# Input statistics placed at another silu, and three of four ring loads issued back to back, in a Mamba and FFN kernel with a planned order

## The chip, the cores and the metric

The kernel runs on one core of one Trainium2 chip. The metric is the device time of one execution in microseconds. Before the change the median of three runs is 4940.54 us (4936.31 to 4943.96).

## What is computed

The input x has 4 sequences of 2048 tokens of 256 numbers. A layer norm is taken, a Mamba block (with a layer norm and a residual of its own) is applied to it and added to x, and a gated feed-forward part follows on another layer norm. Cut to what matters:

```python
def _mamba_block(x, ...):
    residual = x
    xn = (x - mu) * rsqrt(var + 1e-05) * ln_w + ln_b
    xi, z = split(xn @ W_in, 2)                  # 512 channels each
    u = silu(causal_conv(xi, conv_w) + conv_b)   # 4 taps
    dt_r, Bm, Cm = split(u @ W_xproj)            # 16, 64, 64
    delta = softplus(dt_r @ W_dt + b_dt)
    A = -exp(A_log)
    def step(h, inputs):                         # over the 2048 tokens
        dA = exp(d_t[:, :, None] * A)
        h = h * dA + (d_t * u_t)[:, :, None] * B_t[:, None, :]
        return h, einsum('bdn,bn->bd', h, C_t)
    y = (scan(step) + u * D) * silu(z)
    return residual + y @ W_out

x = x + _mamba_block(layernorm(x), ...)
n = layernorm(x)
x = x + (silu(n @ wg.T) * (n @ wu.T)) @ wd.T     # hidden width 768
```

The state has 512 channels times 64 entries, so per token 32768 recurrences run in parallel: 256 rows of 128.

## The kernel before

**Tiling.** The 8192 tokens are cut into 16 blocks of 512 (`NT`, four to a sequence). In a block the 32768 recurrences are 256 pairs (two channels times 64 states on the 128 partitions), in 16 groups of 16. One pair goes through these steps:

- PE spreads delta of two channels over the partitions into one of four `a` buffers in PSUM (line 1528, from the tile `stk`).
- ACT takes the exponential in place, with the pair's row of A as the scale (line 1534).
- DVE runs the recurrence over 512 tokens with one scan instruction (line 1539), in place in a `ring` buffer that holds delta times u times B.

Ahead of the scans, the ring buffer of a group (16 pairs by 512 tokens) is loaded from a scratch tensor `dusc` in DRAM by four loads of four pairs each (`load_du`, line 1494; the first group's first load is split in three), and POOL multiplies it with B in two halves of eight pairs (line 1645). Behind the scans PE contracts the group's states with C (line 1563), and then the buffer is free. There are three ring buffers.

**The dense parts.** While the scans of block n run, the dense work of its neighbours is woven in. In program order it is: `front(n+1)` (load of x, its layer norm, xn and its transposes), `back(n-1)` (gating and output projection), `front_a(n+1)` (projection and convolution), `front_b(n+1)` (the z projection by `project_z`, the silu of u and z at lines 998 to 1001, softplus, the stores for the scans), `back_b(n-1)` (feed-forward, with its silu at lines 1265 to 1267). Silu lies in another table of ACT than the exponential, so each of the two silu stretches begins and ends with a table load, and ACT takes no exponential in between.

**The norm of x.** `layer_norm` with `twice=True` gives the scale and shift of both layer norms in front of the Mamba block from one pair of statistics. Its steps are: four `bn_stats` on DVE (line 491), which read the loaded x and write one of four `bst` buffers each; four `bn_aggr` on DVE (line 492), which write into a PSUM bank `lp`; small ACT steps (two of line 530, lines 540, 541, 542) and three tiny DVE steps (lines 545, 550, 555). x itself stays in a `w4` buffer until it is normalised.

**What sets the order.** No engine order is written by hand. Every instruction is an `op` with a planned cost, and `Planner.run` puts them one by one on PE, ACT, DVE, POOL and SP as it simulates the engines; the resulting orders are emitted, and an instruction waits on the chip only for what its data need. Instructions of the scan chain have kind "S"; dense ones have kind "D" and a `step` at which they are due, spread over the block by cost (`dense`, line 1628): being early or late by some steps shifts a candidate's planned time by at most 170 ns later or 230 ns earlier (`bias`, line 222). Buffers are given out in turns: the four `w4` buffers in program order over everything, the four PSUM `ps` banks in program order among the dense instructions, which also need two free ones (`allocatable`, line 155). In `w4`, the turns of a block are x, xn, xnT, the residual of `back`, two z buffers, then the residual of `back_b` (loaded at line 1224), its xn, xT and the second part of the hidden tile.

All transfers are issued by SP in one order, and a transfer that must wait holds up those behind it. `wire` is the planned time at which everything issued so far has been moved. Transfers of kind "S", the ring loads and the `stk` loads, are not planned earlier than 3 us before that (lines 238 and 239, `AHEAD` = 3000 ns); dense transfers have no such rule. The four loads of a ring buffer are also chained by `after=[last["du"]]`, each behind the start of the one before.

Of the kernel before, what the change touches and what calls it, by code (L numbers as in the profile page):

```python
# [93 lines left out]
class Planner:  # L94
# [114 lines left out]
    def run(self, mul):  # L209
# [17 lines left out]
        while left:  # L227
            best = None
            for e, now in clock.items():
                pick = None  # L230
                cands = []
                due = 1e18
                for o in self.ready[e]:
                    t = self.allocatable(o, 2)
                    if t is None:
                        continue
                    t = max(now, o.est, t)
                    if e == "SP" and o.kind == "S":
                        t = max(t, wire - AHEAD)
                    if o.kind == "S":  # L240
                        due = min(due, t)
                    cands.append((o, t))
                for o, t in cands:
                    late = HOLD if e in HOLD_ON and o.kind != "S" and t + o.cost > due + HOLD_TOL else 0.0
                    sc = (t + bias(o) + late, o.idx)
                    if pick is None or sc < pick[0]:
                        pick = (sc, t, [o])
                if self.ready["MUL"] and (e == "POOL" or e == "DVE" and min(o.idx for o in self.ready["MUL"]) < self.dve_mul):
                    m = min(self.ready["MUL"], key=lambda o: o.idx)
                    whole = m.key[0][0] == 0 or MUL_SET == sum(o.key[0] == m.key[0] for o in self.ready["MUL"])  # L250
                    if e == "POOL":
                        ms = sorted(
                            (o for o in self.ready["MUL"] if o.key[0] == m.key[0]), key=lambda o: o.idx
                        )
                        ms = [o for i, o in enumerate(ms) if o.key[2] == m.key[2] + i]
                        sc = 0.0
                    else:
                        ms = [m]
                        sc = max(LAG, min(MUL_LEAD, SLOPE * (m.step - MUL_MARGIN - cur)))
                    t = max(now, max(o.est for o in ms))  # L260
                    sc = (t + sc, m.idx)
                    if whole and (pick is None or sc < pick[0]):
                        pick = (sc, t, ms)
                if pick and (best is None or pick[1] < best[1]):
                    best = (e, pick[1], pick[2])
            assert best, "no instruction can be placed"
            e, t, os = best
            if os[0].eng == "MUL":
                cost = 88 + 1092 * len(os) if e == "POOL" else 690
                mul(e, os)  # L270
                clock[e] = end = t + cost
                busy[e] += cost
                for o in os:
                    self.ready["MUL"].remove(o)
                    o.eng = e
                    self.commit(o, t, end)
                left -= len(os)
                continue
            o = os[0]
            self.ready[e].remove(o)  # L280
            cost, times = o.cost, 1
            if e == "PE":
                i = int(t / TICK)
                if cols.get(i - 1, 0) < WARM:
                    cost *= 2
                if was == "decay" and o.key == "narrow":
                    cost += SWITCH
                was = o.key
                n = o.cols or o.cost * 2.4
                while recent and recent[0][0] < t - TICK:  # L290
                    recent.popleft()
                if o.key == "decay" and sum(c for _, c in recent) < KEEP:
                    times = 2
                    cost *= 2
                    n *= 2
                recent.append((t + cost, n))
                i = int((t + cost) / TICK)
                cols[i] = cols.get(i, 0) + n
            if e == "SP":
                clock[e] = t + 625  # L300
                wire = max(wire, t + 1275) + o.cost
                end = wire + 985
                busy[e] += o.cost
            else:
                clock[e] = end = t + cost
                busy[e] += cost
            if o.key == "scan":
                cur += 1
            self.commit(o, t, end)
            for _ in range(times):  # L310
                o.fn()
            left -= 1
# [26 lines left out]
def mamba_ffn_kernel(  # L339
# [124 lines left out]
            one(s)  # L464
        return sums

    def layer_norm(src, blocks=range(4), twice=False, sums=None):

# [17 lines left out]

        def stats(j, s):
            st = buf("bst")  # L490
            op("DVE", 326, lambda: nc.vector.bn_stats(st.t, tok(src)[:, s, :]), [(src, s // 2)], [st])
            op("DVE", 205, lambda: nc.vector.bn_aggr(mv()[:, j, :], st.t), [st], [(lp, 0, j)])

        def spread(s):
# [277 lines left out]
    def front(n):  # L772
        r = n % R
        xt = load_x(n) if n else x0
        rs, nm = layer_norm(xt, twice=True)
        rp = buf("s4")
        op("ACT", 180, lambda: nc.scalar.activation(rp.t[:, 0:4], rs.t[:, 0:4], AF.Copy, bias=1.0), [rs], [rp])
        xn = buf("w4")
        normalise(xn, xt, (rs, nm), o=4)

        def keep():
            normalise(xt, xt, (rp, nm))
            store(rsum[r], lambda: tok(xt), 524288, halves(xt), [("rsum", r)])

        if n:
            keep()
        else:
            last["keep"] = keep
        xnT = buf("w4")

        def ev_t(c):
            def ev(ps):
                op(
                    "ACT", act(T, True, 2),
                    lambda: nc.scalar.activation(  # L795
                        xnT.t[:, c, :], ps.t, AF.Identity, bias=lnb[:, c : c + 1], scale=lnw[:, c : c + 1]
                    ),
                    [ps, "lnw", "lnb"], [(xnT, c)],
                )

            return ev

        for c in range(2):
            transposes(xn, c, ev_t(c))
        rest[n] = xnT
# [66 lines left out]
    def project_z(n):  # L872
        xnT = rest[n][0]
        szs = gates[n] = [buf("w4"), buf("w4")]

        def ev_z(k):
            def ev(ps):
                op(
                    "ACT", act(T, True), lambda: nc.scalar.copy(szs[k // 2].t[:, k % 2, :], ps.t),
                    [ps], [(szs[k // 2], k % 2)],  # L880
                )

            return ev

        for k in range(4):
            project(win, DI + k * P, xnT, ev_z(k), ["win"])

    def mix(n):
        r = n % R
# [98 lines left out]
    def front_b(n):  # L988
# [2 lines left out]
        uk = [(u, k) for k in range(4)]  # L991
        if n:
            project_z(n)
            szs = gates[n]
            zk = [(z, k) for z in szs for k in range(2)]

            def silu():
                nc.scalar.activation(u.t, u.t, AF.Silu)
                for h in range(2):
                    nc.scalar.activation(szs[h].t, szs[h].t, AF.Silu)  # L1000
                nc.scalar.preload_act_table_set(EXP_LN)

            o = op("ACT", 6400, silu, uk + zk, uk + zk)
            o.tail = -1283.0
            for k in uk:
                o.tails[k] = -3250.0
        else:

            def silu_a():
                nc.scalar.activation(u.t[:, 0:3, :], u.t[:, 0:3, :], AF.Silu)  # L1010

            def silu_b():
                nc.scalar.activation(u.t[:, 3, :], u.t[:, 3, :], AF.Silu)
                nc.scalar.preload_act_table_set(EXP_LN)

            op("ACT", 2900, silu_a, uk[0:3], uk[0:3])
            op("ACT", 1900, silu_b, uk[3:4], uk[3:4]).tail = -1283.0
# [461 lines left out]
    def group(G):  # L1479
# [14 lines left out]
        def load_du(a, m):  # L1494
            src = dusc[r][h][:, row + a : row + a + m, :].rearrange("d p t -> d (p t)")
            o = load(
                lambda: ring.t[:, a : a + m, :].rearrange("p a t -> p (a t)"),
                src[None, :, :].to_broadcast([64, 2, m * T]),
                m * 262144,
                r=[("dusc", r, h, 0), ("dusc", r, h, 1)],  # L1500
                w=keys[a : a + m] + heads[(a + 3) // 4 : (a + m + 3) // 4],
                after=[stl] if G == 0 and a == 4 else [last["du"]] if "du" in last else [],
            )
            last["du"] = o

        def mul(p):
            o = op("MUL", 0, None, [b2, keys[p]], [keys[p]], step=G * 16 + p)
# [210 lines left out]
```

## Time and profile before

| What | us |
|---|---|
| median of three runs | 4940.54 |
| profiled execution, time | 4944.55 |
| profiled execution, span | 4942.8 |
| DVE busy | 4734.0 |
| POOL busy | 4695.2 |
| PE busy | 4433.3 |
| ACT busy | 4005.2 |

The span is the time from the first to the last instruction of the profiled execution; the time of that execution is 1.75 us longer. A row of the groups names line, engine, operation and tiles, then the count, the busy time, the mean duration in ns, and the idle time of the engine just ahead of these instructions with what ended most of it. Scans overlap a little: one lasts 1198 ns, and they follow each other at 1115 ns. In a timeline, the columns are start and length in us, and a bracket tells how long the engine had been idle and what released it. "issue" as a releaser means that the profile shows no wait.

Some further groups that the text refers to:

| Group | count | busy us | mean ns |
|---|---|---|---|
| line 491, `bn_stats`, DVE | 68 | 23.9 | 410 |
| line 492, `bn_aggr`, DVE | 68 | 11.7 | 171 |
| line 998, table load, ACT | 15 | 19.2 | 1283 |
| line 998, silu of u, ACT | 15 | 28.7 | 1911 |
| line 1000, silu of z, ACT | 30 | 29.8 | 1041 |
| line 1265, silu of the gate, ACT | 15 | 28.7 | 1913 |

| Transfer | count | KB | median us from issue to landing |
|---|---|---|---|
| ring<-dusc | 1023 | 1024 | 7.9 |
| stk<-dsc | 256 | 96 | 5.9 |
| szd<-w | 32 | 512 | 11.6 |
| qd<-w | 32 | 512 | 9.5 |
| w<-rsum | 31 | 512 | 8.3 |

### The profile page before, as it was taken

What the parts mean: (1) busy time and instruction counts of PE and PEld (TensorE: products, weight loads), DVE (VectorE), ACT (ScalarE), POOL (GpSimd) and SP (SyncE); (2) the same over time, 40 slices, a digit from 0 to 9 for tenths busy, and PEclk for the clock granted to TensorE, in tenths of its full rate; (3) what the DMA queues carried; (4) which work ended last, traced back from release to release, by engine and by line L of the source; (5) the groups of instructions that cost most, each with busy time, mean ns of one, the idle gap of its engine ahead of it and who ended that gap; (6) DMA issues with size and microseconds to landing.
All of it is one profiled execution on the core that took longest, in us unless ns stands there. A gap on an engine that the chain in (4) does not pass through costs nothing. (4 is left out here: it accounts for less than half of the span.)

```text
span 4942.8 us, 116006 instructions
## 1 busy us (share of the span) xinstructions
PE 4433.3 (90%) x46924; PEld 2205.2 (45%) x46924; DVE 4734.0 (96%) x4576; ACT 4005.2 (81%) x7378; POOL 4695.2 (95%) x862
## 2 busy tenths in 40 slices
PE   7889989998988999989999899989989999898888
PEld 3434444444444444444444444444444444444435
DVE  7999999999999999999999999999999999999996
ACT  6788878778788887888878788887878878888774
POOL 6999999999999999999999999999998999999994
PEclk9999999999999999999999999999999999999999
DMA  8676776667766777677667676677776767676762
GB/s 295 237 282 252 284 272 266 265 242 287 265 266 257 272 266 280 263 266 279 262 264 278 259 277 255 263 291 267 274 263 247 280 265 282 255 290 253 264 248 86
DMA packets 306347, 1299.87 MB, mean 263 GB/s; under 512 B 33617, under 2 KB 134737, under 8 KB 174866
## 3 DMA queue, kind: packets, MB, share of 16 engines
q1 hardware_dynamic: 305810, 1292.44, 68.6%
q8 instruction: 369, 6.05, 0.5%
q14 instruction: 168, 1.38, 0.1%
HBM read 1186.94 MB, written 105.38 MB: 261 GB/s over the span
## 5 line engine op out<-in xcount | busy, mean ns | idle before, releaser
L1539 DVE TENSOR_TENSOR_SCAN ring<-a,ring 128x512 f32<-128x512 f32 x4096 | 4594.2, 1198 | 103.7 <-ACT a L1534 81.2
L1645 POOL TENSOR_TENSOR ring<-ring,b 128x4088 f32<-128x4088 f32 (+2 forms) x512 | 4540.0, 8897 | 154.3 <-DMA ring<-dusc 116.9
L1534 ACT ACTIVATE a<-a,a 128x512 f32<-128x512 f32 x4096 | 2702.2, 666 | 677.2 <-PE a L1528 647.1
L1528 PE MATMUL a<-stk,selb 128*128 128x512 bf16 x5088 | 1809.3, 391 | 407.4 <-DVE ring L1539 374.7
L1563 PE MATMUL ps<-ring,cz 128*32 128x128 f32 x32768 | 1235.9, 280 | 19.4 <-issue 12.4
L1528 PEld LDWEIGHTS <-selb 128*128 128x128 bf16 x5088 | 471.2, 98 | 1347.6 <-issue 1274.2
L1563 PEld LDWEIGHTS ps<-ring,cz 128*32 128x32 f32 x32768 | 811.1, 110 | 541.4 <-issue 478.0
L596 PE MATMUL ps<-w,wgu 128*128 128x512 f32 x720 | 373.5, 600 | 0.0
L1584 ACT COPY mm<-ps 128x512 f32<-128x512 f32 x512 | 304.5, 596 | 37.2 <-PE ps L1563 36.3
L1597 PE MATMUL ps<-mm,exs 128*32 128x128 f32 (+1 forms) x4112 | 285.3, 407 | 1.3 <-ACT mm L1584 1.0
L596 PE MATMUL ps<-w,win 128*128 128x512 f32 x512 | 260.7, 594 | 0.3 <-ACT w L795 0.3
L830 PE MATMUL ps<-xi,w 128*128 128x512 f32 x480 | 245.8, 593 | 0.0
L1597 PEld LDWEIGHTS ps<-mm,exs 128*32 128x32 f32 x4112 | 116.8, 118 | 202.8 <-ACT a L1534 81.6
L1148 PE MATMUL ps<-wd,w 128*128 128x256 f32 x720 | 195.8, 386 | 0.0
L596 PEld LDWEIGHTS ps<-w,wgu 128*128 128x128 f32 x720 | 138.1, 192 | 111.2 <-issue 58.5
L1148 PEld LDWEIGHTS ps<-wd,w 128*128 128x128 f32 x720 | 132.4, 189 | 42.1 <-issue 14.7
L949 PE MATMUL ps<-w,ident 128*128 128x512 f32 x248 | 133.3, 620 | 6.7 <-ACT ps L944 5.9
L596 PEld LDWEIGHTS ps<-w,win 128*128 128x128 f32 x512 | 96.8, 190 | 89.7 <-issue 57.5
L1148 PE MATMUL ps<-wout,w 128*128 128x256 f32 x480 | 128.4, 388 | 0.9
L830 PEld LDWEIGHTS ps<-xi,w 128*128 128x128 f32 x480 | 88.9, 188 | 82.6 <-issue 62.2
L571 ACT ACTIVATE w<-w,s,s 128x256 f32<-128x256 f32 x192 | 112.8, 597 | 0.9 <-DVE s L555 0.9
L1255 POOL TENSOR_TENSOR w<-w,w 128x512 f32<-128x512 f32 x90 | 113.4, 1281 | 0.0
(154 smaller groups left out, 2416.9 us busy)
## 6 DMA issues: line engine op xcount, KB each, us to landing
ring<-dusc SPq DMA_DIRECT2D x1023, 1024.0 KB, 7.9
stk<-dsc SPq DMA_DIRECT2D x256, 96.0 KB, 5.9
qd<-w SPq DMA_DIRECT2D x32, 512.0 KB, 9.5
szd<-w SPq DMA_DIRECT2D x32, 512.0 KB, 11.6
dusc<-w SPq DMA_DIRECT2D x63, 256.0 KB, 6.4
dsc<-pk SPq DMA_DIRECT2D x63, 256.0 KB, 6.5
rsum<-w SPq DMA_DIRECT2D x31, 512.0 KB, 6.8
w<-rsum SPq DMA_DIRECT2D x31, 512.0 KB, 8.3
```

The source lines that it names most:

```text
L596: lambda ps: nc.tensor.matmul(ps, w[:, c, o : o + P], xT.t[:, c, :], start=(c == 0), stop=(c == 1)),
L830: lambda: nc.tensor.matmul(ps.t, dg.t[:, j * P : (j + 1) * P], xi.t[:, j : j + T], start=(j == 0), stop=(j == 3)),
L949: lambda: nc.tensor.matmul(ps.t, m, t.t, start=False, stop=True, skip_group_check=True),
L1148: lambda ps: nc.tensor.matmul(ps[:, (s % 2) * DM : (s % 2 + 1) * DM], src(k)[:, s * P : (s + 1) * P], w[:, k, :], start=False, stop=(k == ...
L1255: "POOL", 1230, lambda: nc.gpsimd.tensor_tensor(hm(k), hm(k), up.t, ALU.mult),
L1528: "PE", 216, lambda: nc.tensor.matmul(a.t, selb[:, p, :], stk.t, start=True, stop=True),
L1534: lambda: nc.scalar.activation(a.t, a.t, AF.Exp, scale=a2f[:, idx : idx + 1]), [a, "a2"], [a],
L1539: nc.vector.tensor_tensor_scan(v, a.t, v, 0.0, ALU.mult, ALU.add)
L1563: nc.tensor.matmul(pm.t[cg * 32 : cg * 32 + 32, (r8 % 4) * P : (r8 % 4 + 1) * P], framed(cz, blk), ring.t[:, :, blk * 8 : blk * 8 + 8], st ...
L1584: nc.scalar.copy(mm.t[:, hb * 4 : hb * 4 + 4].rearrange("p r a t -> p (r a t)"), pm.t)
L1597: nc.tensor.matmul(ex.t[jh * 32 : jh * 32 + 32, a * 16 : b * 16], framed(exs, jh * 2 + jl), mm.t[:, a:b, :, jh * 2 + jl], start=(jl == 0), ...
L1645: e.tensor_tensor(v, v, b2.t[:, None, t0:].to_broadcast([P, m, T - t0]), ALU.mult)
```

## The change

It has two parts.

The first moves the load of x and the layer norm's statistics of a block. In `front_b` of block n, right behind the z projection and ahead of the silu in program order, x of block n + 1 is loaded and its `layer_norm` is planned. The statistics may be placed from the start of the last z matmul on. `front(n+1)` then takes the finished scale and shift from a table and starts with the normalising. It applies to blocks 2 to 15; block 0 has no silu of that kind, so block 1 keeps the old place.

The second exempts the later loads of a ring buffer from the rule of 3 us: loads with `a` other than 0 get the key "more", which the planner asks for. The first load of a group and the `stk` load keep the rule.

```diff
@@ class Planner, run @@
-                    if e == "SP" and o.kind == "S":
+                    if e == "SP" and o.kind == "S" and o.key != "more":
                         t = max(t, wire - AHEAD)
@@
-    def layer_norm(src, blocks=range(4), twice=False, sums=None):
+    def layer_norm(src, blocks=range(4), twice=False, sums=None, after=()):
...
         def stats(j, s):
             st = buf("bst")
-            op("DVE", 326, lambda: nc.vector.bn_stats(st.t, tok(src)[:, s, :]), [(src, s // 2)], [st])
+            op("DVE", 326, lambda: nc.vector.bn_stats(st.t, tok(src)[:, s, :]), [(src, s // 2)], [st], after=after)
@@ front @@
         xt = load_x(n) if n else x0
-        rs, nm = layer_norm(xt, twice=True)
+        rs, nm = norms.pop(("in", n), None) or layer_norm(xt, twice=True)
@@ project_z @@
         for k in range(4):
-            project(win, DI + k * P, xnT, ev_z(k), ["win"])
+            last["z"] = project(win, DI + k * P, xnT, ev_z(k), ["win"])[-1]
@@ front_b @@
         if n:
             project_z(n)
+            if n + 1 < NT:
+                xt = load_x(n + 1)
+                norms["in", n + 1] = layer_norm(xt, twice=True, after=[last["z"]])
             szs = gates[n]
@@ group, load_du @@
             last["du"] = o
+            if a:
+                o.key = "more"
```

## The prediction

> **What bounds the kernel now.** I read the page first, then the table of waits, then the timeline around the two long ACT stretches of a block.
>
> From the page, the busy time of each engine and the two costliest groups:
>
> ```profile
> PE 4433.3 (90%) x46924; PEld 2205.2 (45%) x46924; DVE 4734.0 (96%) x4576; ACT 4005.2 (81%) x7378; POOL 4695.2 (95%) x862
> L1539 DVE TENSOR_TENSOR_SCAN ring<-a,ring 128x512 f32<-128x512 f32 x4096 | 4594.2, 1198 | 103.7 <-ACT a L1534 81.2
> L1645 POOL TENSOR_TENSOR ring<-ring,b 128x4088 f32<-128x4088 f32 (+2 forms) x512 | 4540.0, 8897 | 154.3 <-DMA ring<-dusc 116.9
> ```
>
> DVE sets the pace: 4096 scans, and only 4942.8 - 4734.0 = 208.8 us idle in the whole span. POOL is nearly as full, so the waits must say who waits for whom:
>
> ```profile
> DVE ring L1539 <- ACT a L1534: 81.2, 43, 4.9
> ...
> DVE ring L1539 <- POOL ring L1645: 0.3, 1, 0.3
> ...
> POOL ring L1645 <- DMA ring<-dusc: 116.9, 41, 31.6
> ```
>
> (Total us, times, longest.) A scan waited for POOL once, 0.3 us. POOL waits for ring loads, 31.6 us of it once at the start, but its product is there in time anyway. What DVE does wait for is ACT, in waits of up to 4.9 us. The timeline around the silu of a block ahead (line 998) shows why; first DVE, then ACT, then SP:
>
> ```profile
> 2913.82 5.66 DVE L1539 TENSOR_TENSOR_SCAN ring<-a,ring 128x512 f32<-128x512 f32 x5
> 2923.63 3.45 DVE L1539 TENSOR_TENSOR_SCAN ring<-a,ring 128x512 f32<-128x512 f32 x3 [4.16 <-ACT a L1534]
> ```
>
> ```profile
> 2916.52 1.28 ACT L998 ACT_TABLE_LOAD   x1
> ...
> 2921.64 1.28 ACT L1001 ACT_TABLE_LOAD   x1
> ```
>
> ```profile
> 2911.93 0.51 SPq L425 DMA_DIRECT2D ring<-dusc  x1
> 2912.55 0.99 SPq L425 DMA_DIRECT2D stk<-dsc  x1
> 2913.94 0.51 SPq L425 DMA_DIRECT2D ring<-dusc  x1
> 2914.52 0.57 SPq L425 DMA_DIRECT2D w<-rsum  x1
> 2915.21 1.18 SPq L425 DMA_DIRECT2D ring<-dusc  x2
> ```
>
> For 6.4 us ACT makes no exponential. DVE uses up the ones it has, and from S + 2.95 to S + 7.11 (S = 2916.52) it stands still: a hole of 4.16 us. The fifteen holes at line 998 are 2.76 to 4.89 us, 62.6 us together. On SP, other transfers go between the four loads of one ring. The other silu of a block (line 1265), on DVE, and its last occurrence, which has no next block:
>
> ```profile
> 2403.10 6.77 DVE L1539 TENSOR_TENSOR_SCAN ring<-a,ring 128x512 f32<-128x512 f32 x6
> 2409.79 1.38 DVE L491 BATCH_NORM_STATS2 bst<-w 128x6 f32<-128x256 f32 x4
> 2412.85 2.34 DVE L1539 TENSOR_TENSOR_SCAN ring<-a,ring 128x512 f32<-128x512 f32 x2 [1.68 <-ACT a L1534]
> ```
>
> ```profile
> 4741.36 2.34 DVE L1539 TENSOR_TENSOR_SCAN ring<-a,ring 128x512 f32<-128x512 f32 x2 [3.04 <-issue]
> ```
>
> This is the view that decides. The four statistics (line 491) **already lie in a hole**: 1.68 + 1.38 = 3.06, the 3.04 of a silu without them. Only their aggregations lie on the path, some 85 us later:
>
> ```profile
> 2494.24 0.16 DVE L492 BATCH_NORM_AGGREGATE ps<-bst 128x2 f32<-128x6 f32 x1
> 2494.31 1.19 DVE L1539 TENSOR_TENSOR_SCAN ring<-a,ring 128x512 f32<-128x512 f32 x1
> 2495.42 0.17 DVE L492 BATCH_NORM_AGGREGATE ps<-bst 128x2 f32<-128x6 f32 x1
> 2495.49 1.19 DVE L1539 TENSOR_TENSOR_SCAN ring<-a,ring 128x512 f32<-128x512 f32 x1
> 2496.60 0.39 DVE L492 BATCH_NORM_AGGREGATE ps<-bst 128x2 f32<-128x6 f32 x2
> 2496.90 2.32 DVE L1539 TENSOR_TENSOR_SCAN ring<-a,ring 128x512 f32<-128x512 f32 x2
> ```
>
> From 2494.24 to 2496.90 are 2.66 us with two scans of pitch 1.115 (four aggregations between them): 2.66 - 2.23 = 0.43 us a block.
>
> **Part one, the statistics.** No instruction is added or removed. For blocks 2 to 15 the load of x, four statistics, four aggregations and the eight small ACT and DVE steps of the norm move from the start of the next dense part to the silu at line 998. Block 2's four statistics are already in that hole (2.76 us left at 246.7, as 4.14 less 1.38); the thirteen others come from the hole at line 1265. Leaving that one gains nothing: it grows from about 1.5 to 2.9 us. Going into the other costs nothing while it lasts: the start of the trace shows such statistics with three of the four aggregations in 1.75 us (78.17 to 79.92); with a fourth of 0.17 they take 1.9 of the 4.2 us. So what can be gained is the aggregations: 14 x 0.43 = 6.0 us, not the 14 x 1.9 = 27 us that the empty hole suggests. The three tiny DVE steps (0.14 us each) need ACT after the silu and stay on the path.
>
> If the cover is gone, that is, if x lands after S + 7.11, the four statistics go between scans: they add 1.38 a block to the 0.43 paid today, 14 x 1.38 = 19.3 us. x is late from S + 7.11 - 1.92 = S + 5.2 on. Its load takes the turn in the w4 buffers right after the second z buffer, where line 1224's load (w<-rsum) is now: issued at 2914.52, S - 2.0, with 8.3 us to landing (the page's median) it comes at S + 6.3, half too late. In 8 of the 13 blocks the third z copy is 3.3 to 3.5 us ahead of the silu, like here; in five it is some 11 us ahead, and x is in time. What speaks for in time: planned work of about 4.5 us (the load 1344, statistics 2124, small steps 1080 ns) now stands behind z instead of ahead of it in an order that spreads some 200 us over 236 steps, so z falls due about 5 steps, 5 to 6 us, earlier. On PE the last z matmuls are cut off from the first by a burst of line 1563 (at 1999.69 to 2006); a few 1.1-us places are enough to bring them ahead of it, with the load ahead of the ring loads too. That is an estimate.
>
> The x tile also holds one of four w4 buffers through the back of the block, so line 1224's load waits for the last z matmul and the normalise at line 571 (2930.83, S + 14.3) for a szd store (11.6 us from its issue near S + 4.2: S + 15.8). A delay of 1 to 2 us in a chain with room (its last dusc store of one block is issued at 2085.97, the next block's first stk load at 2163.99): I take nothing, and up to 2 us over the run. The mean's bank (lp) comes before line 1024's banks in PSUM turns: line 1024 is late if x is late.
>
> **Part two, the loads.** Three of each group's four loads (c1 to c3; 256 groups) are issued right behind the first, ahead of whatever SP held between them: stk, bcs, qd, szd, dusc, dsc, rsum, x. Nothing is added on the wire. A load of 1024 KB at the 401 GB/s that the window from 2915 to 2924 shows takes 2.6 us, so a transfer that loses its place behind c2 and c3 lands 5.2 us later, behind three 7.8. Gain: POOL waits less, worth 0.3 us steady, and at most 3 us at the start, where DVE is idle 22.7 of the 60 us from 30 to 90. Loss: ACT's waits for a buffer's store or load are 18.5 (yl<-qd), 15.4 (dusc<-w) and 11.2 us (dsc<-pk); were they doubled, DVE would feel about what it feels of ACT outside the silus, 9.5 us. So -3 to +10; I take 0, since the first loads, which POOL's first half needs, hardly move, and stk lands 8.9 us or more ahead of its first matmul once the first group is past.
>
> What a page says on the order of transfers is a check on this: the row is the 96-KB stk load with 5.9 us to landing, so it is the queue that takes the time. The Trainium skill (DMA: Bandwidth & Descriptors, section on queues, rings and completion order) says that each DMA engine consumes a queue's descriptors in ring order. By it a load of x behind c1 to c3 can't overtake them and the sum is +19; by the row of w<-rsum alone, placed among the ring loads, it is between -6 and +8.
>
> **The sum.** The profiled run took 4944.55 us (span 4942.8), 4.0 above the median of 4940.54. 4944.55 - 6.0 + 0 = 4938.5; against the median 4934.5. Forecast: **4935 us**, its own range 4927 to 4943.
>
> **The rivals.** *x comes late* (slower). At the silu of line 998 the load stands behind c1 to c3, lands after S + 7.1, and the statistics lie between scans while line 1265's hole stays empty. With the phases of today in 8 blocks: 8 x 1.38 - 6 x 0.43 = +8.5, 4949; in all: +19.3, 4960. It decides from a landing at S + 5.2. For it: part two itself, and the eight blocks. Against: z falls due earlier. I take 4953.
>
> *Statistics ahead of the silu.* If x is early and the dense part is late, the statistics go before the silu, between scans: 1.38 + 0.43 on the path, of which a fuller stock of exponentials (one scan, 1.1) comes back: 0.7 against 0.43 today, 14 x 0.27 = +4, 4944.
>
> *A shorter hole.* DVE does only 2.4 to 3.1 us of scans after S, though four a buffers hold 4.46. Should the new order start the silu with one exponential more in stock, that is 14 x 1.1 = 15 us on top of 6: 4919. For it: holes differ by 0.7 us among blocks by their phase. Against: today's order never reaches it.
>
> **How the numbers follow.** Chances: forecast 0.40, late 0.34, ahead 0.10, shorter 0.16. No change is within 0.2%, 9.9 us, about what a measurement of this kernel can tell. The forecast gives 0.16 of its 0.40 to faster (with gains of part two and a reshuffled order, below 4930.6) and 0.24 to same; late 0.32 slower and 0.02 same; ahead 0.08 same, 0.02 slower; shorter 0.16 faster. So faster 0.32, same 0.34, slower 0.34. The range goes from 4916, just below the shorter hole, to 4962, late in all blocks with part two's small losses: less than one in ten is left out on each side.
>
> **What would show it.** Right: at line 998 statistics and aggregations inside the hole, which leaves about 2.3 us; at line 1265 holes of about 3; no aggregation between scans. Wrong: line 491 between scans right after line 1001, with the load of x landing beyond S + 7; or holes at line 998 under 1.5 us; or DVE waiting for POOL or PE for stk, which would mean that part two is not neutral.

## The result, and the profile after

| Kernel | median us | ratio to the kernel before, 95% interval |
|---|---|---|
| before | 4938.43 | |
| after | 5070.25 | 1.0266 (1.0253 to 1.0279) |

With a fourth run the median of the kernel before is 4938.43 us instead of 4940.54. The change costs 131.8 us. Lines behind 994 have moved down by three and five: the silu of the block ahead is at lines 1001 to 1004, the feed-forward's at 1268 to 1270, the scan at 1544, its exponential at 1539, POOL's product at 1650.

The page of the changed kernel: busy times of the engines, and DVE's busy tenths over the span.

```profile
PE 4419.6 (87%) x46638; PEld 2223.2 (44%) x46930; DVE 4739.6 (94%) x4576; ACT 4007.4 (79%) x7378; POOL 4695.8 (93%) x862
...
DVE  7999899999989989999998999999999898999996
```

DVE does the same work (4739.6 us against 4734.0) and stands still 5062.5 - 4739.6 = 322.9 us instead of 208.8. Six slices, spread over the span, fall from nine tenths to eight. The granted clock of PE is lower too (0.964 against 0.976), but a scan lasts what it did (1199 ns against 1198), and the largest wait for PE, ACT's for the spread delta (line 1528, now 1533), fell from 647.1 us to 636.0; so the clock is not what costs the time. What ACT waits for, first before the change, then after (total us, times, longest), and then what DVE waits for after it:

```profile
ACT w L942 <- DMA dusc<-w: 15.4, 11, 3.6
...
ACT pk L956 <- DMA dsc<-pk: 11.2, 8, 3.9
```

```profile
ACT w L942 <- DMA dusc<-w: 90.3, 20, 7.8
ACT pk L956 <- DMA dsc<-pk: 45.8, 7, 10.5
```

```profile
DVE ring L1544 <- ACT a L1539: 113.6, 76, 5.4
DVE w L957 <- ACT x L961: 41.4, 22, 10.5
...
DVE ps L545 <- ACT ps L542: 31.7, 16, 2.7
DVE w L957 <- ACT pk L956: 27.1, 14, 5.6
```

Both ACT lines are in softplus. Each takes a buffer that a store to DRAM still reads, so ACT waits for that store to land: 136.1 us in all, against 15.4 + 11.2 = 26.6 before. DVE's multiplication at line 957 then waits for ACT 68.5 us (17.7 before), and the scans wait more too. The 31.7 us at line 545 are no loss: nearly all of them lie inside the silu's hole, as will be seen.

Where DVE stands still, summed from the idle time in front of its instructions in each trace. "Silu" is around the table loads, "softplus" from 7 to 105 us behind the start of the silu of the block ahead, "start" the first 100 us, "end" the last 70:

| us | start | silu | softplus | rest | end |
|---|---|---|---|---|---|
| before | 34.7 | 86.0 | 16.7 | 27.2 | 40.6 |
| after | 36.5 | 85.6 | 149.2 | 7.7 | 40.6 |

The softplus stretch loses 132.5 us, the rest gives 19.5 back, and nothing else moves by over 2 us (the span grew by 119.7). In the softplus stretch DVE is idle for 4 to 15 us in 13 of the 15 blocks and for about 1 in the other two. One place of it in the changed kernel's timeline (start, length; in brackets the idle time before and who ended it), SP first, then ACT, then DVE:

```profile
1774.50 2.48 SPq L425 DMA_DIRECT2D ring<-dusc  x4
```

```profile
1782.92 0.33 SPq L428 DMA_DIRECT2D dusc<-w  x1
1783.34 0.38 SPq L425 DMA_DIRECT2D stk<-dsc  x1
1784.54 0.37 SPq L428 DMA_DIRECT2D dsc<-pk  x1
```

```profile
1782.94 0.26 ACT L962 COPY x<-w 128x64 f32<-128x64 f32 x1
...
1789.96 0.63 ACT L942 ACTIVATE w<-w 128x512 f32<-128x512 f32 x1 [5.44 <-DMA dusc<-w]
1790.50 0.64 ACT L1539 ACTIVATE a<-a,a 128x512 f32<-128x512 f32 x1
```

```profile
1782.81 4.55 DVE L1544 TENSOR_TENSOR_SCAN ring<-a,ring 128x512 f32<-128x512 f32 x4
1791.17 2.34 DVE L1544 TENSOR_TENSOR_SCAN ring<-a,ring 128x512 f32<-128x512 f32 x2 [3.80 <-ACT a L1539]
```

The four loads of a ring buffer go out in one go, as part two wants. By the trace the last of them lands at 1789.30, and the small transfers issued behind it follow in the order of their issue: the dusc store at 1789.88, stk at 1790.12, the dsc store at 1790.80. ACT needs the store's buffer for its next instruction and stands still until 1789.96, 5.44 us. Its last exponential ended at 1784.00 and the next ends at 1791.14; of these 7.14 us DVE bridges 3.36 with the scans it still has (to 1787.36) and waits 3.80 us. Over the run a dusc store takes 9.4 us from issue to landing (6.4 before), and 26 of the 63 are issued while all four loads of a group are under way; before, none.

At the silu of the block ahead (here S = 1731.05) it went as predicted:

```profile
1731.82 0.73 DVE L491 BATCH_NORM_STATS2 bst<-w 128x6 f32<-128x256 f32 x2
1732.46 0.40 DVE L492 BATCH_NORM_AGGREGATE ps<-bst 128x2 f32<-128x6 f32 x2
1732.77 0.39 DVE L491 BATCH_NORM_STATS2 bst<-w 128x6 f32<-128x256 f32 x1
1733.08 1.20 DVE L1544 TENSOR_TENSOR_SCAN ring<-a,ring 128x512 f32<-128x512 f32 x1
1734.21 0.16 DVE L492 BATCH_NORM_AGGREGATE ps<-bst 128x2 f32<-128x6 f32 x1
1734.28 0.39 DVE L491 BATCH_NORM_STATS2 bst<-w 128x6 f32<-128x256 f32 x1
1734.59 1.20 DVE L1544 TENSOR_TENSOR_SCAN ring<-a,ring 128x512 f32<-128x512 f32 x1
1735.71 0.16 DVE L492 BATCH_NORM_AGGREGATE ps<-bst 128x2 f32<-128x6 f32 x1
1738.60 0.17 DVE L545 SCALAR_TENSOR_TENSOR ps<-ps,s 128x8 f32<-128x8 f32 x1 [2.73 <-ACT ps L542]
```

All four statistics and aggregations are done before DVE would have run dry, so the hole shrinks to 2.73 us; the other silu's hole, now empty of them, is 2.59 in this block.

```profile
1861.17 0.47 DVE L1461 TENSOR_TENSOR ps<-ps,a 128x128 f32<-128x128 f32 x2
1864.22 3.45 DVE L1544 TENSOR_TENSOR_SCAN ring<-a,ring 128x512 f32<-128x512 f32 x3 [2.59 <-ACT a L1539]
```

### The profile page after: what moved, and what is told of

It is laid out like the page before. It is cut to its first block, busy times and chain, and to the rows that moved or that the text cites. A ratio compares the mean times of both kernels' runs of the same rounds, so it can differ in the third digit from the quotient of the medians.

```text
span 5062.5 us, 115820 instructions
## 1 busy us (share of the span) xinstructions
PE 4419.6 (87%) x46638; PEld 2223.2 (44%) x46930; DVE 4739.6 (94%) x4576; ACT 4007.4 (79%) x7378; POOL 4695.8 (93%) x862
## 5 line engine op out<-in xcount | busy, mean ns | idle before, releaser
L1650 POOL TENSOR_TENSOR ring<-ring,b 128x4088 f32<-128x4088 f32 (+2 forms) x512 | 4546.7, 8948 | 261.9 <-DMA ring<-dusc 155.0
L1544 DVE TENSOR_TENSOR_SCAN ring<-a,ring 128x512 f32<-128x512 f32 x4096 | 4597.9, 1199 | 156.5 <-ACT a L1539 113.6
L1539 ACT ACTIVATE a<-a,a 128x512 f32<-128x512 f32 x4096 | 2697.8, 665 | 711.9 <-PE a L1533 636.0
L1533 PE MATMUL a<-stk,selb 128*128 128x512 bf16 x4816 | 1755.0, 393 | 435.6 <-DVE ring L1544 398.2
L1568 PE MATMUL ps<-ring,cz 128*32 128x128 f32 x32768 | 1251.3, 283 | 40.4 <-issue 8.1
L1568 PEld LDWEIGHTS ps<-ring,cz 128*32 128x32 f32 x32768 | 823.0, 111 | 565.0 <-issue 486.2
L1602 PEld LDWEIGHTS ps<-mm,exs 128*32 128x32 f32 x4112 | 116.9, 118 | 207.9 <-ACT a L1539 93.0
## 6 DMA issues: line engine op xcount, KB each, us to landing
szd<-w SPq DMA_DIRECT2D x32, 512.0 KB, 10.7
```

The lines of the kernel that those rows point to most:

```text
L1533: "PE", 216, lambda: nc.tensor.matmul(a.t, selb[:, p, :], stk.t, start=True, stop=True),
L1539: lambda: nc.scalar.activation(a.t, a.t, AF.Exp, scale=a2f[:, idx : idx + 1]), [a, "a2"], [a],
L1544: nc.vector.tensor_tensor_scan(v, a.t, v, 0.0, ALU.mult, ALU.add)
L1568: nc.tensor.matmul(pm.t[cg * 32 : cg * 32 + 32, (r8 % 4) * P : (r8 % 4 + 1) * P], framed(cz, blk), ring.t[:, :, blk * 8 : blk * 8 + 8], st ...
L1602: nc.tensor.matmul(ex.t[jh * 32 : jh * 32 + 32, a * 16 : b * 16], framed(exs, jh * 2 + jl), mm.t[:, a:b, :, jh * 2 + jl], start=(jl == 0), ...
L1650: e.tensor_tensor(v, v, b2.t[:, None, t0:].to_broadcast([P, m, T - t0]), ALU.mult)
```

## Why ACT waits: what the planner believed

The planner simulated both kernels to the same end, 4892.4 us before and 4891.4 after (its own clock). So the chip does something that it doesn't know. The wire is the smaller part of it: set on the trace's time by the nearest scan, the planner has the dusc store of the example landing at 1788.29, 1.6 us early, and it has line 942 start 4.05 us ahead even of that; the two make 5.6, and ACT waited 5.44 us. The larger part comes from here, where a placed instruction gives up its buffers (`Planner.commit`):

```python
b.left -= 1
if not b.left:
    self.free[b.tag].append((end, o.eng, b.slot))
```

`end` is the end of the user that was placed last, not the latest end of all users. The softplus' `w` (one of four `w2` buffers) is read by the dusc store and by the small copy into x0 at line 962. If the copy is placed last, the buffer counts as free when the copy ends, 0.26 us after it began, though the store lands some 7 us later. The chip waits for the store; the planner has meanwhile given the buffer to line 942 of the next softplus. The one `pk` buffer has the same fault with its dsc store and the matmul at line 967. Counted in the planner's own times, buffers given out ahead of the landing of the store that reads them, by how much in total (a few other places, 31.1 us after the change, are left out):

| | w2 at line 942 | pk at line 956 |
|---|---|---|
| before | 8 times, 8.9 us | 3 times, 6.7 us |
| after | 17 times, 72.0 us | 6 times, 33.5 us |

The fault is in both kernels. The change lets it bite: after it, buffers are given out too early more often, and by more.

## The experiments

In the first four expectations, theory W is this account in an early form; theory F in the later ones is the same account after their results. All ratios are against the kernel before on the same chip.

**Part one alone** (the key "more" left out) and **part two alone** (the loads of a group unpaced, the statistics where they were):

```diff
-            if a:
-                o.key = "more"
```

> Part one alone: statistics of x at the silu of the block ahead, ring loads as before. Theory W (part two makes the softplus stores land late, so that ACT stops in front of buffers that they still read): waits of line 942 on dusc stores and of line 956 on dsc stores stay near the 15.4 and 11.2 us of before, time 4925 to 4955. Rival P (part one does the harm: the x tile held in a w4 buffer and the norm's PSUM bank hold up the dense part): 5020 or more.

> Part two alone: statistics as before, the last three ring loads exempt from the 3 us. Theory W: lines 942 and 956 wait over 100 us together, time 5030 to 5080. Rival P: within 20 us of before, 4920 to 4960. If both parts are needed, between the two.

Measured: part one alone 5006.83 us, ratio 1.0137 (1.0122 to 1.0152); part two alone 5029.52, 1.0185 (1.0170 to 1.0200). ACT's waits of part one alone, then of part two alone:

```profile
ACT w L942 <- DMA dusc<-w: 75.0, 21, 6.5
...
ACT pk L956 <- DMA dsc<-pk: 24.6, 7, 5.6
```

```profile
ACT pk L956 <- DMA dsc<-pk: 61.6, 9, 13.5
...
ACT w L942 <- DMA dusc<-w: 30.7, 10, 7.8
```

Part two came out just short of what theory W expected, on both counts (these waits 92.3 us instead of over 100, the time 5029.5 instead of 5030 or more). Part one met no expectation: it leaves the ring loads paced (a dusc store takes 7.2 us to land, 6.4 before), and was still 70 us slower, with the same two waits. So unpaced loads are not the cause but one way to it; a new order of the dense work is another. This spoke for the free list, which any new order can trip. The planner's own times, counted as in the table, agree: with part one alone line 942 gets its buffer too early 19 times, by 53.5 us, and line 956 5 times, by 16.0; with part two alone 10 times, by 22.0, and 7 times, by 46.5. In DVE's idle time both have 96 us in softplus (96.2 and 96.6). The two losses, 70 and 93, do not add up to 132, probably because the same few buffers are hit.

**The free list mended**, in the changed kernel and in the kernel before:

```diff
             b.left -= 1
+            if end >= b.last[0]:
+                b.last = (end, o.eng)
             if not b.left:
-                self.free[b.tag].append((end, o.eng, b.slot))
+                self.free[b.tag].append((*b.last, b.slot))
```

> Both parts, and the planner gives a buffer free at the latest planned end among its users, not at the end of the user that it placed last. Theory W says that the planner put line 942 ahead of the store's landing because it took the end of a later placed ACT copy: the waits of lines 942 and 956 on stores fall below 40 us together, time 4925 to 4965. Rival R (the landings themselves are later than planned, or another resource is short): waits stay over 100 us and the time over 5040.

> The kernel before with the same change of when a buffer counts as free. Theory W: its 15.4 and 11.2 us of such waits fall below 10 us together; DVE felt only part of them, so 4920 to 4945. Rival R: no change of the waits, time as before.

Measured: changed kernel 4923.07 us, 0.9971 (0.9960 to 0.9981); kernel before 4931.38, 0.9992 (0.9983 to 1.0002). The changed kernel's waits (lines moved by three more):

```profile
ACT pk L959 <- DMA dsc<-pk: 7.0, 3, 2.5
ACT w L945 <- DMA dusc<-w: 6.9, 4, 3.4
```

136.1 us of waiting became 13.9, DVE's idle time in softplus fell from 149.2 to 15.5, and 147.2 us of time went; the time is 2 us below what theory W expected. In the planner's own times no buffer is given out ahead of a landing any more. In the kernel before, the same mend is worth at most a few us.

**Is it the free list, or only another order?** A mended planner reorders much. So the planner's code was left as it was in the changed kernel, and the store alone was planned behind the copy that reads its buffer, so that it is the last placed:

```diff
-            store(dusc[r][h][i], lambda: w.t, 262144, [w], [("dusc", r, h, i)])
+            seen = []
...
-                op("ACT", 180, lambda: nc.scalar.copy(x0.t[:, 1, :, i], w.t[:, 0:1].to_broadcast([P, 64])), [w], [(x0, 1, i)])
+                seen.append(op("ACT", 180, lambda: nc.scalar.copy(x0.t[:, 1, :, i], w.t[:, 0:1].to_broadcast([P, 64])), [w], [(x0, 1, i)]))
+            store(dusc[r][h][i], lambda: w.t, 262144, [w], [("dusc", r, h, i)], after=seen)
```

The second kernel does the same for the store of pk: `last["pk"]` is the matmul of line 967.

```diff
-            [("dsc", r, h, i)],
+            [("dsc", r, h, i)], after=[last["pk"]],
```

> The changed kernel whole, the planner as it was; only the store of w to dusc is planned behind the copy of x0 that reads the same buffer, so that the store is the buffer's last planned user and its landing is what the free list keeps. The wait for pk is left as it is. Theory F: the wait of ScalarE's absolute value for the store of w falls from 90 us to under 20, the one of its copy for the store of pk stays at 30 to 55, and the time is 4955 to 5000 us. The rival (the mended free list only reshuffled the order, and the place of a store against a copy is no cause): still 5040 us or more.

> As the run before it, and the store of pk is planned behind the second matmul that takes pk off (the one buffer's last other reader) too, the planner's code untouched. Theory F: both waits are under 15 us together and the time is 4915 to 4935 us, as with the mended free list (4923). The rival (something else in the unpaced loads or the moved statistics costs by itself): 4960 us or more, with the waits for these stores gone.

Measured: with the store of w alone 4955.34 us, 1.0035 (1.0021 to 1.0048); with both 4921.09, 0.9965 (0.9953 to 0.9977). ACT's waits, first with one, then with both:

```profile
ACT pk L956 <- DMA dsc<-pk: 45.2, 5, 11.8
...
ACT w L942 <- DMA dusc<-w: 6.0, 5, 3.0
```

```profile
ACT pk L956 <- DMA dsc<-pk: 9.2, 5, 3.8
...
ACT w L942 <- DMA dusc<-w: 0.2, 1, 0.2
```

Each wait goes with its own store, and the other stays (45.8 and 45.2). The planner's own times say the same: with the store of w moved, line 942 gets no buffer too early, and line 956 still 5 times, by 32.4 us; with both, none does. Two changes of plan that leave the planner's code as it is give the time of the mended free list within 2 us. This settles the cause.

**What the two parts are worth without the fault:** part one alone, and part two alone, each with the mended free list.

> Part one alone (the statistics moved, the ring loads paced as before), with the planner's free list keeping the latest end of a buffer's users. Theory F (the planner gives a store's buffer out before the store lands, and that alone made the changed kernel slow): ScalarE's waits at the softplus' copy and absolute value for the stores of w and pk fall from 75 and 25 us (part one alone) to under 12 together, and the time is 4915 to 4930 us, under the kernel before by about what the 14 hidden aggregations are worth (6 us) and with the planner mended as well. Theory M (moving the statistics disturbs the order of the softplus by itself, whatever the free list says): over 4960 us.

> Part two alone (three of a group's four ring loads unpaced, the statistics where they were), with the free list keeping the latest end. Theory F: the unpaced loads cost little once the planner knows when a store's buffer is free: 4925 to 4945 us, within 10 us of the kernel before with the same mend (4931), against 5030 without it. A rival (the wire itself is the loss: stores behind unpaced loads are late whatever is planned): over 4970 us, with the store waits still over 60 us.

Measured: part one 4899.76 us, 0.9920 (0.9906 to 0.9933), the fastest of all; part two 4956.20, 1.0036 (1.0022 to 1.0050). Against the kernel before with the mend (4931.38), part one gains 31.6 us, 15 beyond the end of what was expected (store waits 13.8 us, where under 12 were), and part two costs 24.8, outside the expected 10, but 14 us below the rival's 4970 and with store waits of 15.0 us where the rival has over 60. On top of part one, part two costs 23.3 (4899.76 to 4923.07). The profile of part one with the mend:

```profile
PE 4372.4 (89%) x46606; PEld 2208.4 (45%) x46902; DVE 4730.2 (96%) x4576; ACT 4004.9 (82%) x7378; POOL 4695.9 (96%) x862
...
DVE  7999999999999999999999999999999999999996
```

DVE's idle time, by place, shows where the parts act:

| us, free list mended | silu | softplus | rest |
|---|---|---|---|
| before | 86.5 | 9.7 | 23.6 |
| part one | 84.1 | 9.3 | 3.9 |
| part two | 91.5 | 25.4 | 21.7 |
| both | 86.0 | 15.5 | 9.9 |

Alone, part two loses 15.7 us in the softplus and 5.0 around the silus; on top of part one it loses 6.2 in the softplus, 6.0 in the rest and 1.9 around the silus. No single wait carries it. Part one's gain lies in the rest, over half of it from 190 to 250 us behind the silu (15.2 to 3.5 us). Over the whole rest, DVE's waits at what was line 1116 go from 9.5 us to 1.5, those of scans for an exponential from 7.2 to 0.2. (The profiled executions are 23.5 us apart, their medians 31.6.)

The planner foresaw part of this. Its simulated end is 4902.3 us for the mended kernel before, 4884.8 with part one and 4908.6 with part two: 17.5 of the 31.6 us gained, and 6.3 of the 24.8 lost.

**The second load of x.** The issues of the kernel before have 15 loads of x of 512 KB; those of the changed kernel:

```profile
w<-in SPq DMA_DIRECT2D x29, 512.0 KB, 10.7
```

`front` still calls `load_x`, so x of 14 blocks is loaded twice, once for the statistics and once to be normalised. A kernel with part one and the mend keeps the first x and holds its w4 buffer:

```diff
-        xt = load_x(n) if n else x0
+        xt = norms.pop(("x", n), None) or (load_x(n) if n else x0)
...
                 norms["in", n + 1] = layer_norm(xt, twice=True, after=[last["z"]])
+                norms["x", n + 1] = xt
```

> As part one with the mended free list (4900 us), but the next block's front takes the x that was loaded for the statistics instead of loading it a second time: 15 loads of x instead of 29, and the tile stays in one of the four w4 buffers through the rest of the block, as the prediction had thought of the change. If the second load costs as much as its 512 KB on the wire in front of transfers that are waited for (1.3 us at 401 GB/s, 14 times 1.3 = 18 us), the time is 4880 to 4892. If it is hidden and the held buffer costs the 1 to 2 us a run that the prediction gave it, 4897 to 4905. If holding the buffer through the block delays the dense part, over 4908; then the second load is what makes part one pay.

Measured: 4918.28 us, 0.9959 (0.9946 to 0.9973), 18.5 slower than with the second load (on another chip; by the two ratios it is 19). So the load that moves 7.3 MB more pays for itself. That it does so by setting the w4 buffer free is likely and not shown, since the planner makes a new order of everything. Its simulated end rises by 3.3 us only (4884.8 to 4888.1). In the traces ACT's waits for a w4 buffer that a store to rsum still reads go from 3.3 us to 12.0, and DVE's idle time in the softplus from 9.3 to 16.7. Part one with one load gains 13.1 us against the mended kernel before (16 by the ratios); the planner's end gains 14.2, and the aggregations were put at 6.0.

## Why the prediction was wrong

- **DVE sets the pace; the statistics only trade one hole for another:** right. The holes at the silu of the block ahead shrank from 62.8 us (the prediction has 62.6) to 44.1 in all, the rest of what is idle around the silus, the feed-forward's above all, grew from 86.0 - 62.8 = 23.2 to 85.6 - 44.1 = 41.5. All 56 aggregations of blocks 2 to 15 now lie in that silu's stretch, none between scans elsewhere.
- **x comes late** (the main rival): wrong, and rightly put second. In the eleven blocks whose landing the trace has, x for the statistics lands between S - 0.3 and S + 1.0, ahead of the S + 5.2 from which it would cost.
- **"No instruction is added or removed":** wrong. The diff leaves `load_x` in `front`, and 14 loads are added. The step priced the held buffer at up to 2 us; with the mended planner the kernel that holds it is 18.5 us slower than the one that loads twice. The error had no hand in the result, since the changed kernel does not hold the buffer.
- **The size of part one, 6.0 us:** too small. It is 31.6 without the fault, 13.1 for the version that the step described. The sum had only the aggregations in it, and left out what a new order of the dense work does elsewhere.
- **Part two, "I take 0", between -3 and +10:** this is the step that failed. It had the right wait (ACT for dusc<-w and dsc<-pk, 26.6 us) and multiplied it by two; it became 136.1, five times as much, and DVE felt not 9.5 us more but, in the softplus, 132.5. Part two alone makes it 92.3 and costs 93 us. Three things were missed. The first is the cause: the planner gives a store's buffer out too early, in the kernel before 11 times by 15.6 us at these two lines, after the change 23 times by 105.5, and the prediction did not look at when it counts a buffer as free. Second, the size of a wait of today was taken for the size of what may come, though the planner allows a store's buffer to be used ahead of its landing by as much as the landing is away: the bound should have been the landing itself, 5 to 8 us behind two or three loads, for each of the some 60 softplus that can be hit. Third, four exponentials in stock last 4.5 us (four scans of 1.115). The waits before are 3.9 us at most; after, 18 of the 27 are over 4.5 us, and what is beyond the stock reaches DVE. With 23 us, part two without the fault would still have been outside the bound of +10.
- **Part one had no price in the softplus at all.** Alone it costs 70 us with the fault, and none of the rivals says so: they asked when x lands, not what else a new order touches.
- **POOL and stk:** right. stk takes 7.9 us to land instead of 5.9 and POOL waits 155.0 us for ring loads instead of 116.9, but scans waited 1.4 us for POOL in all, and PE once for stk, 2.7 us.
- **The order of transfers:** the prediction set the page's rule (the Trainium skill, DMA: Bandwidth & Descriptors, section on queues, rings and completion order) beside the load of x, where it cost nothing. The example above agrees with it at another place: the store landed 0.58 us behind the last of the four loads issued ahead of it. Of the 1664 transfers whose landing the trace of before has, and the 1676 of after, none landed ahead of one issued before it.

Of the three rivals none had the mechanism. The time lies 108 us above the upper end of the range.

## What to carry to other kernels

Where a planner orders the work, look up when it takes a buffer for free, and compare that with what the chip waits for: a reader that ends late but is placed early (a store) must keep the buffer. Bound the cost of a later transfer by its own delay times the places that could wait for it, not by a multiple of today's waits. An engine that feeds the bottleneck may stand still for as long as the stock between them lasts; what is beyond that is lost. Count from the last result ahead of the wait to the first behind it (7.14 us in the example, for a wait of 5.44), against the stock that is left at that moment (3.36), not against a full one.

## What the runs showed of the hardware

With 14 more loads of 512 KB the mended kernel of part one was 18.5 us faster than with the buffer held; the wire had room for them (q1's packets took 69.8% of the 16 DMA engines' span with them, 69.1% without). How long a 256-KB store takes to land goes with the ring loads of 1024 KB under way when it is issued. Among those whose landing the trace has, the median to dusc in the changed kernel is 2.0 us with none (12 stores), 7.1 with two (11) and 10.7 with four (15); in the kernel before 2.6 with none (8), 6.5 with two (23), and none was found behind four. The median over all stores to dusc went from 6.4 to 9.4 us, with part two alone to 6.7 only.
